# A rounding step and a product moved from VectorE to ScalarE in a kernel's last stage, with a new order of its turn

## The chip, the cores and the metric

The kernel runs on one core of a Trainium2 chip. The time is the device time of one execution in microseconds (us). The engines are called by the profile's names: PE (TensorE), DVE (VectorE), ACT (ScalarE), POOL (GpSimd), SP (SyncE, which only issues transfers here).

## The reference, cut to what matters

Four residual layers, each fed by a group norm without weights, run over 32 images of 128 channels by 32 x 32:

```python
x = x + conv3x3(gn(x))                # layer 0
x = x + mamba_block(gn(x))            # layer 1: two passes, forwards and backwards
x = x + attention(gn(x))              # layer 2
x = x + circuit(gn(x))                # layer 3
...
# layer 2: means over rows and columns go through two small mambas to maps
result_h = sigmoid(a_h) * x_y
result_w = sigmoid(a_w) * x_x
out1 = _c1x1(concatenate([result_h, result_w], axis=1), adjust_w)
return x * out1
...
# layer 3: a small quantum circuit on four angles per pixel
xq = xf @ pre_w.T + pre_b
z = _simulate(xq, q_weights)
out = z @ post_w.T + post_b
```

A group of the norm has four channels. Its mean and variance are means over four partitions, got with a small product by a constant matrix (`self.group`). The circuit's state is written with sines of sums of the angles, so its work per pixel is: a product to turns, the whole part of the turns taken off (rounding), a sine, a product, a square, a product.

## The kernel before, in words

`run()` (L1068) has three stages. `images()` (L1116) does layers 0 and 1, image after image, in an order written out by tables (`PLACES`, `DECAYS`, `LEADS`): 128 scan directions of 32 steps each. At an image's end (L1245) `total` writes the new image to a DRAM tensor `x2`, `rows` and `columns` sum it, three statistics stages give the norm of layer 2, and `means` (L1278) scales the sums on ACT (L1286) and sends the small tile `st` (72 columns) to the DRAM tensor `stats` (L1289). The tiles of one image, `st` among them, come from the pool `img`; the weights from the pool `par`. Both pools end with this stage.

Then `run()` opens a pool `maps` on the right side of SBUF, loads all of `stats` into the tile `means` (L1106, on SP's queue), and calls `attention()` (L1343): two more scan directions over the means of all images at once. Its parameters lie in a pool `par2`, and are loaded in `Mamba.__init__` (L309): five loads per mamba on ACT's queue (L320), one weight and four rows on SP's (L322, L325), products of them on DVE (L328), an exponential on ACT (L331). Its first products on PE are those of `project` (L396), which read `means`; ACT reads their result (L403, recorded at L960).

`tail()` (L1606) is the last stage: the multiplication of layer 2 by its maps, and layer 3. It is a pipeline written by hand: the list `order` (L1757) names 22 parts with the number of turns by which each lags behind the first. Turn j runs the parts in the list's order, each on image j less its lag, so 32 images take 40 turns. The instructions of an engine run in the order in which they are written. By engine, in the list's order:

- PE: `adjust(0)`, `angles`, `states`, `mean`, `adjust(1)`, `outputs`, `variance`
- DVE: `end` (two passes), `root` (one column), `adjusted(0)`, `sums` (three), `less` (one column), `rounded` (two passes, L1719 and L1720), `spread` (three of one column, L1685 to L1687), `turns`, `adjusted(1)`
- ACT: `normed`, `squares`, `normal`, `sines`
- POOL: `total` (L1670), `root`'s power (L1697), `outer` (two products over 128 x 1024, rh at L1644 and rw at L1645)
- SP: the load of the next image (L1639), and the output at `end` (L1753)

Inside one turn `mean` needs `sums`, `spread` needs `mean`, `variance` needs `spread`. `root`, in the next turn, needs `variance`; `less` and `normal` follow it. `rounded` needs `angles`, `turns` needs `rounded`, `sines` needs `turns`. `total` needs `adjusted(1)` of the turn before. The two halves of `adjust` have a PSUM bank each; `q`, `psi`, `mean` and `variance` have one each.

Of the kernel before, what the change touches and what calls it, by code (L numbers as in the profile page):

```python
# [12 lines left out]
F32 = mybir.dt.float32  # L13
BF16 = mybir.dt.bfloat16
AF = mybir.ActivationFunctionType
ALU = mybir.AluOpType
# [3 lines left out]
P = 128  # L20
S = 32
HW = S * S
L = S + 3
# [3 lines left out]
MAGIC = 12582912.0  # L27
# [912 lines left out]
class Kernel:  # L940
# [127 lines left out]
    def run(self):  # L1068
        tc, nc, d = self.tc, self.nc, self.d
        with ExitStack() as ctx:  # L1070
            cst = ctx.enter_context(tc.tile_pool(name="cst", bufs=1))
            self.dram = ctx.enter_context(tc.tile_pool(name="dram", bufs=2, space=bass.MemoryType.DRAM))
            cbig = cst.tile([P, 2 * P], F32, name="cbig")
            nc.sync.dma_start(cbig, d["cbig"])
            self.group, self.ident = cbig[:, :P], cbig[:, P:]
            self.sel = cst.tile([3 * DS, DS, P], BF16, name="sel")
            nc.sync.dma_start(self.sel, d["sel"])
            self.half = cst.tile([P, P], BF16, name="half")
            nc.vector.tensor_copy(self.half, self.ident)
            self.ones = cst.tile([P, 1], F32, name="ones")  # L1080
            nc.sync.dma_start(self.ones, d["ones"])
            self.vecs = cst.tile([P, len(VEC)], F32, name="vecs")
            nc.scalar.dma_start(self.vecs, d["vec"])
            self.eps = cst.tile([P, 1], F32, name="eps")
            nc.vector.memset(self.eps, 1e-5)
            self.one = cst.tile([P, 1], F32, name="one")
            nc.vector.memset(self.one, 1.0)
            self.less = cst.tile([P, 1], F32, name="less")
            nc.vector.memset(self.less, -1.0)
            self.part = cst.tile([P, 1], F32, name="part")  # L1090
            nc.vector.memset(self.part, 1.0 / S)
            self.power = cst.tile([P, 1], F32, name="power")
            nc.vector.memset(self.power, -0.5)


            self.stats = self.dram.tile([P, self.n, 2 * L + 2], F32, name="stats", bufs=1)
            self.x2 = self.dram.tile([self.n, P, HW], F32, name="x2", bufs=1)
            with ExitStack() as scans:
                self.work = Work(scans.enter_context(tc.tile_pool(name="work", bufs=1)))
                self.psm = scans.enter_context(tc.tile_pool(name="psm", bufs=2, space=PSUM))  # L1100
                self.psb = scans.enter_context(tc.tile_pool(name="psb", bufs=2, space=PSUM))
                self.psy = scans.enter_context(tc.tile_pool(name="psy", bufs=1, space=PSUM))
                self.images()
                right = ctx.enter_context(tc.tile_pool(name="maps", bufs=1, side="right"))
                self.means = right.tile([P, self.n, 2 * L + 2], F32, name="means")
                nc.sync.dma_start(self.means, self.stats)  # L1106
                self.maps = right.tile([P, self.n, 4 * S], F32, name="maps")
                self.attention()
            self.tail()
# [6 lines left out]
    def images(self):  # L1116
        tc, nc, d = self.tc, self.nc, self.d
        with ExitStack() as ctx:
            par = ctx.enter_context(tc.tile_pool(name="par", bufs=1))
            img = ctx.enter_context(tc.tile_pool(name="img", bufs=2))  # L1120
            w0 = par.tile([P, 9, P], F32, name="w0")
            nc.sync.dma_start(w0, d["w0"])
            nin = par.tile([P, 2, P], F32, name="nin")
# [121 lines left out]
            def end(im):  # L1245
                def inner(c):
                    def run():
                        assert im.outs == 4
                        cs = slice(c * 512, (c + 1) * 512)
                        ps = self.mm()  # L1250
                        nc.tensor.matmul(ps, nin[:, 1], im.o[:, cs], start=True, stop=True)
                        self.later(
                            lambda: nc.scalar.activation(
                                im.o[:, cs], ps, AF.Relu, bias=bn[1][1], scale=bn[1][0]
                            )
                        )
                    return run

                def total():
                    nc.gpsimd.tensor_tensor(im.xt, im.xt, im.o, ALU.add)  # L1260
                    nc.sync.dma_start(
                        self.x2[im.idx : im.idx + 1].rearrange("a p l -> p (a l)"), im.xt
                    )
                    im.st = img.tile([P, 2 * L + 2], F32, tag="means", name="st")
                    nc.gpsimd.memset(im.st, 0.0)

                def rows():
                    nc.vector.tensor_reduce(
                        im.st[:, 3:L], im.xt.rearrange("p (h w) -> p h w", w=S), AX.X, ALU.add
                    )  # L1270

                def columns():
                    nc.vector.tensor_reduce(
                        im.st[:, L + 3 : 2 * L], im.xt.rearrange("p (h w) -> p w h", w=S),
                        AX.X, ALU.add,
                    )

                def means():  # L1278

                    st, mv = im.st, im.st[:, 2 * L :]  # L1280
                    to = img.tile([P, 2], F32, tag="gn_to", name="gn_to")
                    nc.gpsimd.tensor_tensor(to[:, 0:1], mv[:, 1:2], self.part, ALU.mult)
                    nc.gpsimd.tensor_tensor(to[:, 1:2], mv[:, 0:1], mv[:, 1:2], ALU.mult)
                    nc.gpsimd.tensor_tensor(to[:, 1:2], to[:, 1:2], self.less, ALU.mult)
                    both = st[:, : 2 * L].rearrange("p (a l) -> p a l", a=2)[:, :, 3:]
                    nc.scalar.activation(  # L1286
                        both, both, AF.Identity, bias=to[:, 1:2], scale=to[:, 0:1]
                    )
                    nc.sync.dma_start(self.stats[:, im.idx], st)  # L1289

                stats = self.stats_stages(lambda: im.xt, img, lambda: im.st[:, 2 * L :])
                return [
                    *(Stage(inner(c), pe=0.9, act=0.8, takes=True, gap=2 - c) for c in range(2)),
                    Stage(total, pool=2.4, gap=2), Stage(rows, dve=1.3, gap=2),
                    Stage(columns, dve=1.3), *stats, Stage(means, act=0.3, pool=0.6, gap=2),
                ]

            images, ways, plan = [], [], Table(self)
            for j in range(self.n):
                im = Image()  # L1300
# [305 lines left out]
    def tail(self):  # L1606
        tc, nc, d = self.tc, self.nc, self.d
        with ExitStack() as ctx:
# [54 lines left out]
            def adjusted(c):  # L1663
                def run(im):
                    xn = im.xn[:, halves[c][1]]
                    nc.vector.tensor_tensor(xn, xn, im.adj[c], ALU.mult)  # L1666
                return run
# [14 lines left out]

            def spread(im):
                im.mv, im.dv = tile_([P, 2], "gn_mv"), tile_([P, 1], "gn_dv")
                nc.vector.tensor_copy(im.mv[:, 0:1], im.ps[:, 0:1])  # L1685
                nc.vector.tensor_tensor(im.dv, im.ag[:, 0:1], im.mv[:, 0:1], ALU.subtract)  # L1686
                nc.vector.scalar_tensor_tensor(  # L1687
                    im.dv, im.dv, im.dv, im.ag[:, 1:2], ALU.mult, ALU.add
                )
# [7 lines left out]
                nc.gpsimd.tensor_tensor(im.mv[:, 1:2], im.dv, self.power, ALU.pow)  # L1697

            def less(im):
                mv = im.mv  # L1700
                nc.vector.scalar_tensor_tensor(  # L1701
                    mv[:, 0:1], mv[:, 0:1], -1.0, mv[:, 1:2], ALU.mult, ALU.mult
                )

            def normal(im):
                mv = im.mv
                im.x4 = tile_([P, HW], "x4")
                nc.scalar.activation(im.x4, im.xt, AF.Identity, bias=mv[:, 0:1], scale=mv[:, 1:2])

            def angles(im):  # L1710
                im.q = bank("q", 1)
# [5 lines left out]
            def rounded(im):  # L1717
                im.kk = tile_([64, 512], "kk")
                nc.vector.tensor_scalar(im.kk, im.q[:64], wb, MAGIC, ALU.add, ALU.add)  # L1719
                nc.vector.tensor_scalar(im.kk, im.kk, MAGIC, None, ALU.subtract)  # L1720

            def turns(im):
                im.rr = tile_([64, 512], "rr")
# [24 lines left out]
            def end(im):  # L1748
# [7 lines left out]

            order = [  # L1757
                (total, 3), (adjust(0), 2), (end, 8), (normed, 1), (root, 5), (angles, 6),
                (adjusted(0), 2), (states, 7), (squares, 7), (sums, 4), (less, 5), (normal, 5),
                (mean, 4), (outer, 1), (rounded, 6), (adjust(1), 2), (spread, 4), (turns, 6),  # L1760
                (sines, 6), (outputs, 7), (adjusted(1), 2), (variance, 4),
            ]
            with tc.manual_schedule():
                for j in range(self.n + 8):
# [25 lines left out]
```

## Time and profile before

| | us |
|---|---|
| median of 3 runs | 12554.25 |
| lowest and highest | 12554.06, 12565.31 |
| the profiled execution's own time | 12567.35 |
| its span | 12565.6 |
| L1289, last `st` sent | 11987.75 |
| L1106, `means` asked for | 11989.32 |
| first product of the last stage's maps, rh (L1644) | 12255.6 |
| last output issued (L1753) | 12562.0 |

The profile is one execution. Its times count from the start of the span. A line of a timeline has start, duration, engine, source line, operation, output and inputs, and the shape; `xN` says how many instructions were merged. An engine's name with a q (ACTq, SPq) stands for the instructions that it only issues. In the groups' lines the number behind the bar is the idle time of the engine just ahead, with what ended it.

### The profile page before, as it was taken

The numbers are of one execution on the slowest core, as the hardware profiler recorded it, in microseconds if no ns is written. First come the engines' busy times: TensorE is split into PE (matmuls) and PEld (weight loads), VectorE is DVE, ScalarE is ACT, GpSimd is POOL, SyncE is SP. The second block draws the span as 40 slices with busy tenths as digits, with TensorE's granted clock in tenths as the row PEclk, the third lists the DMA queues.
The fourth block names the chain that finished last, engine by engine and source line by source line (L and its number), as shares of the span: only waits on it lengthen the run. The fifth ranks groups of instructions, "written<-read, shape, count | busy, mean of one in ns | idle before, by whom it ended". The sixth has DMA issues, their size and how long they took to land. (4 is left out here: it accounts for less than half of the span.)

```text
span 12565.6 us, 211133 instructions
## 1 busy us (share of the span) xinstructions
PE 12230.3 (97%) x76364; PEld 8662.6 (69%) x76364; DVE 12059.9 (96%) x7702; ACT 11859.4 (94%) x23290; POOL 11992.8 (95%) x6399
## 2 busy tenths in 40 slices
PE   8999999999999999999999999999999999999988
PEld 5777777777777777777777777777777777777642
DVE  8999999999999999999999999999999999999978
ACT  7999999999999999999999999999999999999963
POOL 6999999999999999999999999999999999999966
PEclk9999999999999999999999999999999999999989
DMA  4555555555555555555555555555555555555532
GB/s 139 187 185 185 186 186 186 187 183 187 185 187 185 188 184 184 183 186 187 186 186 186 186 185 185 186 189 184 185 185 186 187 185 186 186 185 184 187 135 108
DMA packets 633949, 2278.48 MB, mean 181 GB/s; under 512 B 77480, under 2 KB 81144, under 8 KB 632776
## 3 DMA queue, kind: packets, MB, share of 16 engines
q1 hardware_dynamic: 630600, 2263.08, 51.8%
q8 instruction: 603, 9.88, 0.3%
q14 instruction: 442, 3.62, 0.1%
q10 hardware_dynamic: 2304, 1.90, 0.1%
HBM read 2221.36 MB, written 43.34 MB: 180 GB/s over the span
## 5 line engine op out<-in xcount | busy, mean ns | idle before, releaser
L882 POOL TENSOR_TENSOR hh<-hh,cc 128x1024 f32<-128x1024 f32 x4160 | 9762.8, 2375 | 210.4 <-DVE hh L873 125.9
L873 DVE TENSOR_TENSOR_SCAN hh<-da,bu 128x1024 f32<-128x1024 f32 x4160 | 9288.0, 2273 | 291.1 <-PE y L918 68.1
L857 ACT ACTIVATE but<-dut,bt 128x128 f32<-128x128 f32 x14936 | 4503.0, 394 | 71.5 <-PE bu L830 71.4
L918 PEld LDWEIGHTS y<-cbig,hh 128*128 128x128 f32 x33280 | 3762.4, 141 | 1164.7 <-issue 973.1
L816 ACT ACTIVATE da<-dt,m_na 128x1024 f32<-128x1024 f32 x4096 | 4448.3, 1143 | 29.0 <-DVE hh L873 23.7
L918 PE MATMUL y<-cbig,hh 128*128 128x128 f32 x33280 | 4359.7, 275 | 58.1 <-POOL hh L882 57.7
L830 PE MATMUL bu<-cbig,but 128*128 128x128 f32 x19368 | 2545.4, 275 | 33.2 <-DVE hh L873 26.7
L830 PEld LDWEIGHTS bu<-cbig,but 128*128 128x128 f32 x19368 | 2200.9, 141 | 220.9 <-issue 128.8
L865 DVE TENSOR_TENSOR bu<-du,bu 128x1024 f32<-128x1024 f32 x1739 | 2104.6, 1210 | 83.6 <-PE bu L837 73.9
L396 PE MATMUL mm<-hpad,m_wc 128*128 128x512 f32 x4096 | 1943.5, 603 | 33.4 <-ACT dt L960 25.0
L396 PEld LDWEIGHTS mm<-hpad,m_wc 128*128 128x128 f32 x4096 | 709.7, 190 | 775.6 <-issue 695.4
L837 PE MATMUL bu<-parts,sel 48*128 48x512 bf16 x3478 | 1052.8, 383 | 42.1 <-DVE hh L873 41.2
L854 POOL TENSOR_TENSOR but<-dut,bt 128x1024 f32<-128x1024 f32 x554 | 1063.2, 1919 | 0.0
L524 POOL TENSOR_TENSOR du<-dt,uc 128x1024 f32<-128x1024 f32 x260 | 615.7, 2368 | 36.7 <-ACT dt L960 36.7
L960 ACT ACT_TABLE_LOAD x477 | 612.0, 1283 | 9.3 <-DMA my_cw<-in_my_cw 1.4
L965 ACT ACT_TABLE_LOAD x470 | 603.0, 1283 | 11.8 <-DMA cbig<-in_cbig 3.6
L1170 PE MATMUL mm<-xpad,w 128*128 128x512 f32 x1152 | 542.8, 608 | 2.7 <-ACT xpad L1155 2.7
L897 PEld LDWEIGHTS y<-m_skip,uc 128*128 128x128 f32 x4096 | 489.3, 194 | 50.4 <-issue 23.9
L897 PE MATMUL y<-m_skip,uc 128*128 128x128 f32 x4096 | 514.5, 279 | 1.0 <-ACT back L937 0.9
L417 PE MATMUL mm<-uc,m_xw 128*128 128x512 f32 x1024 | 497.7, 609 | 0.0
L837 PEld LDWEIGHTS <-sel 48*128 48x128 bf16 x3478 | 193.7, 94 | 409.0 <-issue 289.2
L960 ACT ACTIVATE uc<-mm,m_pv 128x512 f32<-128x512 f32 x512 | 335.0, 686 | 109.0 <-PE mm L396 106.0
(208 smaller groups left out, 7364.8 us busy)
## 6 DMA issues: line engine op xcount, KB each, us to landing
cc<-rows SPq DMA_DIRECT2D x4160, 512.0 KB, 4.1
xt<-in_x SPq DMA_DIRECT2D x32, 512.0 KB, 5.7
x<-xt SPq DMA_DIRECT2D x32, 512.0 KB, 2.9
xt<-x SPq DMA_DIRECT2D x32, 512.0 KB, 3.9
out<-xt SPq DMA_DIRECT2D x32, 512.0 KB, 2.9
rows<-dbl SPq DMA_DIRECT2D x130, 64.0 KB, 3.9
stats<-st SPq DMA_DIRECT2D x32, 36.0 KB, 3.5
means<-stats SPq DMA_DIRECT2D x1, 1152.0 KB, 5.6
```

What stands on the lines that cost most here:

```text
L396: nc.tensor.matmul(self.view(ps), m.wc[:, v, j, h * P : (h + 1) * P], self.taps(j, c), start=(j == 0), stop=(j == 3),)
L816: k.nc.scalar.activation(t, w.dt[h], AF.Exp, scale=w.m.na[:, h, n : n + 1])
L830: k.nc.tensor.matmul(t[:, b * P : (b + 1) * P], but[:, b], k.ident, start=True, stop=True, is_transpose=True,)
L837: k.nc.tensor.matmul(t[:, cs], k.sel[:, n], w.parts[:, cs], start=True, stop=True)
L854: engine.tensor_tensor(t, w.dut[h], each, ALU.mult)
L857: engine.activation(t[:, b], w.dut[h][:, b], AF.Copy, scale=w.bt[:, b, n : n + 1])
L865: k.nc.vector.tensor_tensor(t, w.du[h], t, ALU.mult)
L873: k.nc.vector.tensor_tensor_scan(way(t), way(self.da.pop(i)), way(self.bu.pop(i)), 0.0, ALU.mult, ALU.add)
L882: k.nc.gpsimd.tensor_tensor(t, t, self.cc.pop(i), ALU.mult)
L897: nc.tensor.matmul(self.y[g][: w.bl, b], w.uc[h][:, at], m.skip[:, h], start=(b == 0), stop=False)
L918: k.nc.tensor.matmul(self.y[g][: w.bl, b], t[:, at], k.ident, start=False, stop=(n == DS - 1 and b == w.per - 1), is_transpose=True,)
L960: self.nc.scalar.activation(*args, **kw)
```

## The change

In `tail()`: the second pass of `rounded`, which subtracts the rounding constant again, becomes the part `whole`, an activation on ACT with a constant tile `unmagic` as its bias. `less`, the product of the mean and the reciprocal deviation, becomes an activation on ACT with the latter as its scale; the minus sign moves into `spread`, which now writes the negated mean. `spread` subtracts the mean straight from PSUM. The list has another order: `rounded` and `whole` stand ahead of `less`, and `mean` stands behind `adjust(1)`.

Between the first two stages: the pool `img` is opened ahead of `par`; the last image's `st` is taken from the pool `work`, stays in SBUF, and is copied into `means` by POOL; the load of `means` takes the other 31 images.

```diff
+            self.unmagic = cst.tile([64, 1], F32, name="unmagic")
+            nc.vector.memset(self.unmagic, -MAGIC)
...
-            self.stats = self.dram.tile([P, self.n, 2 * L + 2], F32, name="stats", bufs=1)
+            self.stats = self.dram.tile([P, self.n - 1, 2 * L + 2], F32, name="stats", bufs=1)
...
-                nc.sync.dma_start(self.means, self.stats)
+                nc.sync.dma_start(self.means[:, : self.n - 1], self.stats)
+                nc.gpsimd.tensor_copy(self.means[:, self.n - 1], self.last)
...
+            img = ctx.enter_context(tc.tile_pool(name="img", bufs=2))
             par = ctx.enter_context(tc.tile_pool(name="par", bufs=1))
-            img = ctx.enter_context(tc.tile_pool(name="img", bufs=2))
...
-                    im.st = img.tile([P, 2 * L + 2], F32, tag="means", name="st")
+
+                    pool = self.work if im.idx == self.n - 1 else img
+                    im.st = pool.tile([P, 2 * L + 2], F32, tag="means", name="st")
...
-                    nc.sync.dma_start(self.stats[:, im.idx], st)
+                    if im.idx == self.n - 1:
+                        self.last = st
+                    else:
+                        nc.sync.dma_start(self.stats[:, im.idx], st)
...
-                nc.vector.tensor_copy(im.mv[:, 0:1], im.ps[:, 0:1])
-                nc.vector.tensor_tensor(im.dv, im.ag[:, 0:1], im.mv[:, 0:1], ALU.subtract)
+
+                nc.vector.tensor_scalar(im.mv[:, 0:1], im.ps[:, 0:1], -1.0, None, ALU.mult)
+                nc.vector.tensor_tensor(im.dv, im.ag[:, 0:1], im.ps[:, 0:1], ALU.subtract)
...
             def less(im):
-                mv = im.mv
-                nc.vector.scalar_tensor_tensor(
-                    mv[:, 0:1], mv[:, 0:1], -1.0, mv[:, 1:2], ALU.mult, ALU.mult
-                )
+                im.by = tile_([P, 1], "by")
+                nc.scalar.activation(im.by, im.mv[:, 0:1], AF.Copy, scale=im.mv[:, 1:2])
...
-                nc.scalar.activation(im.x4, im.xt, AF.Identity, bias=mv[:, 0:1], scale=mv[:, 1:2])
+                nc.scalar.activation(im.x4, im.xt, AF.Identity, bias=im.by, scale=mv[:, 1:2])
...
-                nc.vector.tensor_scalar(im.kk, im.kk, MAGIC, None, ALU.subtract)
+
+            def whole(im):
+                nc.scalar.activation(im.kk, im.kk, AF.Identity, bias=self.unmagic)
...
-                (adjusted(0), 2), (states, 7), (squares, 7), (sums, 4), (less, 5), (normal, 5),
-                (mean, 4), (outer, 1), (rounded, 6), (adjust(1), 2), (spread, 4), (turns, 6),
-                (sines, 6), (outputs, 7), (adjusted(1), 2), (variance, 4),
+                (adjusted(0), 2), (states, 7), (squares, 7), (sums, 4), (rounded, 6), (whole, 6),
+                (less, 5), (normal, 5), (outer, 1), (adjust(1), 2), (mean, 4), (spread, 4),
+                (turns, 6), (sines, 6), (outputs, 7), (adjusted(1), 2), (variance, 4),
```

## The prediction

> **What bounds the kernel now.** I read the page first, then the stretches of the last part, then the chain, then one turn in order of time. The page:
>
> ```profile
> span 12565.6 us, 211133 instructions
> PE 12230.3 (97%) x76364; PEld 8662.6 (69%) x76364; DVE 12059.9 (96%) x7702; ACT 11859.4 (94%) x23290; POOL 11992.8 (95%) x6399
> ```
>
> These shares describe the scans, which the change doesn't touch. The last part runs from 12255 us to the end, 310 us or 2.5% of the span. Its stretch (columns: PE, PEld, DVE, ACT, POOL busy, clock, DMA share, GB/s) and the chain that ended last:
>
> ```profile
> 12300.00:12400.00 100.00, 84.22 (x251) 27.58 (x250) 98.37 (x172) 40.69 (x46) 74.50 (x45) 1.00 0.32 116
> ```
> ```profile
> 12437.66 1.21 DVE gn_st L1675 x2
> 12439.10 1.48 DVE gn_mv L1701
> 12440.58 0.67 DVE kk L1719
> 12441.27 1.44 DVE kk L1720
> ```
>
> DVE is full, ACT 60% idle. But a one-column product (L1701) costs as much as a pass over 64x512. The timeline of one turn, DVE and POOL, says why:
>
> ```profile
> 12443.80 0.67 DVE L1666 TENSOR_TENSOR xn<-xn,adj 128x512 f32<-128x512 f32 x1
> 12444.61 2.37 POOL L1670 TENSOR_TENSOR xt<-xt,xn 128x1024 f32<-128x1024 f32 x1 [2.18 <-ACT rr L1729]
> ...
> 12446.93 0.55 POOL L1697 TENSOR_TENSOR gn_mv<-gn_dv,power 128x1 f32<-128x1 f32 x1
> 12447.45 1.92 POOL L1644 TENSOR_TENSOR rh<-maps 128x1024 f32<-128x1024 f32 x1
> ...
> 12447.81 1.57 DVE L1701 SCALAR_TENSOR_TENSOR gn_mv<-gn_mv 128x1 f32<-128x1 f32 x1
> ...
> 12449.31 1.92 POOL L1645 TENSOR_TENSOR rw<-maps 128x1024 f32<-128x1024 f32 x1
> ...
> 12450.07 1.44 DVE L1720 TENSOR_SCALAR kk<-kk 64x512 f32<-64x512 f32 x1
> ...
> 12451.80 0.22 DVE L1687 SCALAR_TENSOR_TENSOR gn_dv<-gn_dv,gn_ag 128x1 f32<-128x1 f32 x1
> ```
>
> L1701 ends at 12449.38, when rh ends (12449.37); L1720 ends at 12451.51, just behind rw (12451.23). In the drain, where POOL makes no rh and rw, the same two take 0.11 and 0.42 us (the tiles' own rows: L1720 min 418 ns, median 1439). So a DVE operation with two SBUF inputs, or the plain SBUF pass of L1720, waits until the POOL product under way is over; L1666, L1675, L1719 with PSUM or one SBUF input don't. The turn is a loop: rw ends; L1720 ends 0.28 later; the three small ones to L1687's end at 12452.02 take 0.51; L1724 and the second L1666 end 1.25 later; 0.13 on, POOL's total starts (12453.40). That is 2.17. From total, pow starts after 2.32, rh after another 0.52, rw after 1.86 and runs 1.92: 6.62. 2.17 + 6.62 = 8.79, and total's starts from 12286.32 to 12523.76 are 27 intervals of 8.79. The one wait whose removal shortens a turn is the wait behind rw.
>
> **The tail, part by part.** Removed from DVE: L1701 (1.56) and L1720 (1.44). Added on ACT: the pass over 64x512, 0.62 (sine 0.63, square 0.59 for that shape), and the product, 0.30 (L857, a copy with a column as scale, is 0.394 at 128 columns; less 0.1 for the columns). ACT per turn: 1.23 + 0.59 + 0.62 + 0.30 + 1.24 + 0.63 = 4.6, against 3.7. Only what lies on the loop counts. The copy of the mean becomes a product from PSUM of the same size, and dv now subtracts PSUM, one SBUF input: both at nothing different. But L1687 keeps two SBUF inputs (dv, ag). It is 0.22 alone; in the ramp, where L1686 or L1687 met a running rw, each took up to 1.76 to 1.78. Does it meet one now? I walk the new order with total at 0, rw then at 4.70 to 6.62. On PE the variance product of the turn before goes out when L1687 ends, which the walk must return. Take that at -1.39: adjust(0) runs -1.09 to 0.80 (1.9, from 12443.52 to 12445.42), angles 0.98 and states as much to 2.76, adjust(1) 1.89 to 4.65, then mean. DVE reads mean some 0.45 later (0.42 from its start, at the ramp's first mean) at about 5.1, dv 0.18 later, L1687 near 5.5: 0.8 inside rw. It ends with rw at 6.63. 6.63 less one turn is -1.39 again if the turn is 8.02, so the walk closes. The loop is then 0.02 + 1.25 + 0.13 + 6.62 = 8.02. PE has 7.3 per turn, ACT 4.6, DVE's own work 5.9: they fit. rounded ends near 4.0, whole on ACT 4.7, turns needs it at 6.6: 1.9 us of cover. If it went, each us of lateness would be a us of turn.
>
> Moving mean behind adjust(1) makes DVE wait at spread; queued behind it are turns, adjusted(1) and, through that, POOL's total: just the loop counted. Outputs stand behind mean on PE, and variance behind outputs; before L1687 ends both have time.
>
> Sum: 27 turns by 0.77 = -20.8. Ramp: the interval before them, 7.60, loses the old waits and falls to POOL's own 6.6: -1.0. Drain: the first turn without rh and rw is 6.41 and PE's 7.1 becomes its length, +0.7; the last images meet no POOL product, so ACT's 0.62 and 0.30 replace 0.42 and 0.11, with four crossings of 0.09 between engines and a place behind another image's whole: +1.6. Tail: -19.5.
>
> A rule against the change: the Trainium skill, "ScalarE: Activation LUTs", Rules for kernel authors, wants add and mul on VectorE, not ScalarE. By operation length it is right here: 0.42 against 0.62, 0.11 against 0.30, so 27 turns by 0.4 = +11 us. By the row at its place, 1.44 and 1.56 with the wait, it is wrong. I take the row.
>
> **The hand-over at 11990 us.** Before:
>
> ```profile
> 11975.57 0.36 ACTq L320 DMA_DIRECT2D mx_zw<-in_mx_zw  x1
> ...
> 11987.28 0.44 ACT L1286 ACTIVATE st<-st,gn_to 128x64 f32<-128x64 f32 x1 [2.30 <-POOL gn_to L1284]
> ...
> 11989.28 1.28 ACT L960 ACT_TABLE_LOAD   x1
> ```
>
> means is asked for at 11989.32 on SP, lands 5.6 later, and PE's first projection (L396) starts at 11995.26, its first reader on ACT at 12000.71. The load of 31 images may now go out some 12 us earlier and leaves that path; a POOL copy of 72 columns (some 0.3) brings the last. Behind the load on SP's queue stand loads that it delays by 0.33. But mx_zw's issue waited for the last ACT reader of par (11975.54), though its own place was w0's, read long before: new tiles wait for the whole old pool. With img at the bottom, the attention's parameters wait for img's last reader, L1286, until 11987. So ten parameter loads, table loads and the two exponentials on ACT, hidden until now, follow L1286. Before they took 9.4 us to 11984.98 and 2.8 more after L1286, 12.2; late waits behind other work fall away. From 11986.8 that gives 11998 to 11999 for the first reader instead of 12000.71; PE has by then two of its four projections done (two PSUM buffers) and starts the third at 11998.7 to 12000 instead of some 12004.4. From 0 (all of the chain again exposed) to -6.5 (PE alone, four blocks of 3.5 to 5.4 from 11988.3); I take -4.5. The constant's memset at the start: 0.1, under the first loads.
>
> Sum -24.0. Against the profiled execution's 12567.35 (span 12565.6) that gives 12543; the median of the runs shown is 13.1 lower, and from 12554.25 it is 12530.
>
> **Rivals.** (a) L1687 escapes rw, because mean comes 0.8 us sooner than walked. Then PE bounds, at 7.3 per turn: 27 by 0.7 more, 12511. Against it: PE's 0.98s and 1.89s are steady in every turn. (b) The hand-over gives nothing or loses up to 5 (weights late): 12535 to 12540. For it: all 16 us of the old preparation are moved. (c) Slower: table loads. The product uses Copy between Identity and Sine; the stage had one load for Sine, Identity and Square (L1729, 1283 ns, once), and no row shows Copy beside Sine. If it forced two loads a turn: by the rows a load is 1.28 with no gap behind it (11987.74 to 11989.03), ACT 4.6 + 2.6 = 7.2, under 8.02, costing some 9 in the drain, 12539. The skill, same page, What ACT_TABLE_LOAD costs, has 2.66 with its drain: 4.6 + 5.3 = 9.9, 27 by 1.1 = +30, drain +10 to +20, hand-over -4.5: 12590 to 12600. It decides when ACT's turn passes 8.79, two loads above 4.2 us. The page's Table sets section counts copy among the functions in every set, so unlikely.
>
> **How the numbers follow.** About 0.2% (25 us) is what a measurement of this kernel can tell. Forecast 0.70, split by the hand-over and by the spread of runs (11 us among three) about 12529: 0.38 faster, 0.32 same. (a) 0.08, faster. (b) 0.16, same. (c) 0.06, slower. Faster 0.46, same 0.48, slower 0.06. Range 12508 to 12548: (a) below; (b) plus spread above; (c) left out.
>
> **What would show it.** Total's starts 8.0 apart; L1687's line at some 1.1 us, ending with rw; whole at 0.62, product 0.3 on ACT, one table load; PE busy 91% there; L396 before 11990, mx_zw after 11986. Turns of 7.3 or of 9 and more, or an L1687 of 0.22, would prove the walk wrong.

## The result and the profile after

| | before | after |
|---|---|---|
| median, us | 12556.1 (14 runs) | 12530.36 (14 runs) |
| lowest and highest | 12542.28, 12568.96 | 12524.02, 12545.64 |
| profiled execution, its span | 12567.35, 12565.6 | 12530.45, 12528.7 |

The ratio of after to before is 0.9978, with a 95% interval from 0.997 to 0.9986. The forecast was 12530.0 us. The page's head, and a stretch of the last stage (its length, then the columns PE, PEld, DVE, ACT, POOL, granted clock of PE, DMA share, GB/s):

```profile
span 12528.7 us, 211028 instructions
PE 12221.0 (98%) x76364; PEld 8667.2 (69%) x76364; DVE 12006.1 (96%) x7639; ACT 11889.0 (95%) x23355; POOL 11992.6 (96%) x6400
```
```profile
12300.00:12400.00 100.00, 90.34 (x274) 32.12 (x274) 86.78 (x163) 55.92 (x75) 81.76 (x50) 1.00 0.36 127
```

In this stretch DVE fell from 98 to 87 busy us of 100, and ACT rose from 41 to 56. No engine is full, though PE, at 90, is near it. The chain that ended last:

```profile
12299.22 1.47 DVE gn_dv L1696
...
12307.24 1.46 DVE gn_dv L1696
```

The two DVE waits that the chain of before held (1.48 and 1.44) are gone. A new one stands there: L1696, the last of `spread`'s three one-column operations, comes back every 8.02 us. Part of one turn, in order of time (POOL's last line is the next `total`):

```profile
12402.23 0.72 ACT L1729 ACTIVATE kk<-kk,unmagic 64x512 f32<-64x512 f32 x1 [0.44 <-DVE kk L1726]
...
12403.01 1.90 POOL L1653 TENSOR_TENSOR rw<-maps 128x1024 f32<-128x1024 f32 x1
...
12403.48 1.45 DVE L1696 SCALAR_TENSOR_TENSOR gn_dv<-gn_dv,gn_ag 128x1 f32<-128x1 f32 x1
12404.86 0.73 DVE L1733 SCALAR_TENSOR_TENSOR rr<-q,wb,kk 64x512 f32<-64x512 f32 x1
...
12406.32 2.37 POOL L1678 TENSOR_TENSOR xt<-xt,xn 128x1024 f32<-128x1024 f32 x1 [1.41 <-ACT rr L1738]
```

L1696 starts 0.47 into rw and ends at 12404.93; rw ends at 12404.91. `whole` (L1729) is done at 12402.95 and its reader (L1733) starts at 12404.86, so its cover is 1.9 us. No row says that L1696 waits for POOL. Its length says it, against 0.22 in the drain, where POOL makes no rw, and so does an end that falls on rw's.

The hand-over:

```profile
11975.37 0.44 ACT L1291 ACTIVATE st<-st,gn_to 128x64 f32<-128x64 f32 x1 [10.67 <-POOL gn_to L1289]
11975.84 0.37 ACTq L320 DMA_DIRECT2D mx_zw<-in_mx_zw  x1
11975.84 1.14 DVE L328 TENSOR_TENSOR mx_wc<-mx_uw,mx_cw 128x256 f32<-128x256 f32 x3 [1.82 <-ACT st L1291]
...
11976.37 10.00 PE L396 MATMUL mm<-means,mx_wc 128*128 128x512 f32 x16 [2.55 <-DVE mx_wc L328]
...
11985.83 0.69 ACT L960 ACTIVATE uc<-mm,mx_pv 128x512 f32<-128x512 f32 x1
...
11986.57 7.32 PE L396 MATMUL mm<-means,mx_wc 128*128 128x512 f32 x16 [0.20 <-ACT uc L960]
...
11993.92 0.69 ACT L960 ACTIVATE uc<-mm,mx_pv 128x512 f32<-128x512 f32 x1 [2.86 <-PE mm L396]
```

The parameters' loads now start behind the last image's scaling, as walked. PE's first projection starts at 11976.37, when the product `mx_wc` (L328) is there, which waited for that scaling; POOL's copy (0.50) ends at the same time. PE then works through the four projections (32 products) until 11993.88 and stands for 0.4 us in between.

**Where the 36.9 us between the two spans went.** Three stretches of both traces:

| us | before | after | difference |
|---|---|---|---|
| last ReLU of the images to the fourth read of a projection on ACT | 36.45 | 30.00 | -6.45 |
| from there to the first rh (attention) | 244.4 | 245.2 | +0.8 |
| first rh to the end | 309.96 | 289.54 | -20.4 |

That is -26.1, beside -25.7 between the medians. The other 10.8 us arose ahead of the first row: that ReLU starts at 11974.76 in the one profile and at 11963.92 in the other. The image stage does the same work in both, and in the profiles of the nine kernels below, which share it, the same ReLU starts between 11957.8 and 11971.8, with before's hand-over (11958.2 to 11962.6) no later than with after's; so I take it for the spread of executions. What goes with it is PE's granted clock, which the traces show at 0.50 for stretches of 3.4 us and more. Summed up ahead of that ReLU, it stood there for 184 us before and for 160 after; in the eleven profiles the earliest ReLUs (11957.8 and 11958.2) have 133, the latest below (11971.8) 178. Which of the two is the cause no run shows. A reader of the two spans alone would have credited the 10.8 us to the change.

### The profile page after: what moved, and what is told of

Same layout as the page of the kernel before. It is cut to its first block, busy times and chain, and to the rows that moved or that the text cites. A ratio compares the mean times of both kernels' runs of the same rounds, so it can differ in the third digit from the quotient of the medians.

```text
span 12528.7 us, 211028 instructions
## 1 busy us (share of the span) xinstructions
PE 12221.0 (98%) x76364; PEld 8667.2 (69%) x76364; DVE 12006.1 (96%) x7639; ACT 11889.0 (95%) x23355; POOL 11992.6 (96%) x6400
```

## The experiments

My theory was the prediction's: the stage is a loop through the DVE operation that waits for rw, and nothing else in the edit matters there. The rivals stand in the expectations. Turn means the interval between two starts of `total`; last stage, from the first rh to the end. Of `less` alone, `whole` alone and the order alone there is one run each, so they are read by their turns; the others have several, and a ratio to before with its interval.

**The two halves of the change.** The last stage's edits alone (before's images and hand-over), and the hand-over's alone:

> The changed last stage with the hand-over of before (pool par at the bottom, all of stats loaded). Theory (two independent parts): turns of 8.02 as in the changed kernel, the last stage some 20 us shorter than before, the first projection again waits for the load of means; ratio to before 0.9984, 0.9 to 1.6 us per thousand around it from scatter. Rival (the hand-over carries a good part of the gain): the last stage 10 us shorter at most.

> The last stage of before with the new hand-over (img at the bottom, last tile kept on chip). Theory: last stage unchanged at 310 us with turns of 8.79; from the last image's second ACT pass to the fourth read of the first projections some 6 us less than before; ratio 0.9995. Rival (the hand-over is worth nothing, because the parameters now wait): 0 us there, ratio 1.000.

Measured: the last stage's part 12538.57 us, ratio 0.9983 (0.9976 to 0.999), turn 8.02, last stage 288.7, hand-over 36.9. The hand-over's part 12549.64 us, ratio 0.999 (0.9982 to 0.9998), turn 8.79, last stage 309.65, hand-over 29.9. The halves do not touch each other: each profile shows the new value of its own stretch and the old of the other. The hand-over's gain in the median is barely clear of noise; its 6.5 us in the profile repeats.

**The old order with the moved operations.**

```diff
-  (sums, 4), (rounded, 6), (whole, 6), (less, 5), (normal, 5), (outer, 1), (adjust(1), 2), (mean, 4), (spread, 4),
+  (sums, 4), (less, 5), (normal, 5), (mean, 4), (outer, 1), (rounded, 6), (whole, 6), (adjust(1), 2), (spread, 4),
```

> The changed kernel with the two parts on ACT, but the list in the order of before (mean ahead of adjust(1), less and normal ahead of whole). Theory (the turn is set by where the last DVE operation with two SBUF inputs, in spread, meets POOL): mean is there earlier, that operation meets rh instead of rw and ends with it, then turns waits for whole, which stands behind normal on ACT: walked at 7.64 per turn, last stage 281 us against 289.6, so 9 us faster than the changed kernel. Rival (the new order is what makes the moves pay): turns longer than 8.02, up to 8.8.

Measured: 12524.61 us, ratio 0.9972 (0.9963 to 0.9981), turn 7.62, last stage 283.6. Lines of its turn, and lines of the chain that ended last:

```profile
12384.45 1.90 POOL L1652 TENSOR_TENSOR rh<-maps 128x1024 f32<-128x1024 f32 x1
...
12385.97 0.40 DVE L1696 SCALAR_TENSOR_TENSOR gn_dv<-gn_dv,gn_ag 128x1 f32<-128x1 f32 x1
...
12387.75 0.74 DVE L1733 SCALAR_TENSOR_TENSOR rr<-q,wb,kk 64x512 f32<-64x512 f32 x1 [1.38 <-ACT kk L1729]
```
```profile
12385.25 0.38 PE mean L1689 x2
...
12390.69 0.69 DVE xn L1674
12391.38 1.21 DVE gn_st L1683 x2
...
12392.61 0.22 DVE gn_ag L1685
...
12392.88 0.38 PE mean L1689 x2
```

With `mean` early, L1696 meets the end of rh, waits 0.2, and rw not at all. `turns` (L1733) does wait 1.38 for `whole`, as expected, but 7.64 was walked along the wrong path: `whole` is not in the chain. The chain closes over PE and DVE, once a turn: `mean`, the second half of `adjust`, `outputs`, `variance`, the first half of `adjust` for the next turn, then on DVE `adjusted(0)` and `sums`, and `mean` again. PE stands 0.24 for DVE's sums ahead of `mean`. The work behind `whole` has some room: DVE idles 0.22 for PE ahead of `adjusted(0)`. The new order costs 0.40 us of turn against the old one with the same moves, and 6.0 us of the last stage. In the medians that isn't clear: the two intervals overlap.

**The wait itself taken away.** The new order, but the difference stays in PSUM, in an unused column of the mean's bank, so that L1696 has one SBUF input left:

```diff
-  nc.vector.tensor_tensor(im.dv, im.ag[:, 0:1], im.ps[:, 0:1], ALU.subtract)
-  nc.vector.scalar_tensor_tensor(im.dv, im.dv, im.dv, im.ag[:, 1:2], ALU.mult, ALU.add)
+  nc.vector.tensor_tensor(im.ps[:, 1:2], im.ag[:, 0:1], im.ps[:, 0:1], ALU.subtract)
+  nc.vector.scalar_tensor_tensor(im.dv, im.ps[:, 1:2], im.ps[:, 1:2], im.ag[:, 1:2], ALU.mult, ALU.add)
```

> The changed kernel, with the difference of spread written to PSUM, so that the operation after it reads one SBUF input and one PSUM input. Theory (two SBUF inputs make it wait for POOL's product under way): it takes 0.2 us instead of 1.45, turns fall to PE's own 7.3, last stage 269 us, ratio to before 0.9967. Rival 1 (the operation is long for another reason, its place behind mean or its scalar operand): it stays at 1.4 and turns at 8.0. Rival 2 (PE's or POOL's loop is nearer than walked): 0.2 us, but turns of 7.6 and more.

Measured: 12500.48 us, ratio 0.9955 (0.9942 to 0.9969), turn 7.20, last stage 265.6. Its interval lies below that of the change (0.997 to 0.9986).

```profile
12349.44 1.91 POOL L1653 TENSOR_TENSOR rw<-maps 128x1024 f32<-128x1024 f32 x1
...
12350.33 0.22 DVE L1696 SCALAR_TENSOR_TENSOR gn_dv<-mean,gn_ag 128x1 f32<-128x1 f32 x1
```
```profile
12280.00:12380.00 100.00, 100.00 (x307) 35.70 (x305) 80.08 (x182) 62.20 (x83) 92.40 (x56) 1.00 0.42 148
```

The same operation on the same engine, 0.89 into a running rw, takes 0.22, in all 32 images from 222 to 224 ns. So it isn't POOL's running that costs time, but the second SBUF input. That is what the Trainium skill ("SBUF — State Buffer", Who interferes with whom) says: a DVE instruction with two SBUF inputs and a POOL instruction that reads SBUF exclude each other, and one with a single SBUF input, outside the modes that take both ports, does not.

The column that the operation takes as its scalar moved to PSUM with it; L1701 of before has no such column and waited as well. PE is busy throughout, the chain that ended last lies on PE alone, and the turn is PE's. The last stage is 24 us shorter than with the change.

**Both together, PSUM and the old order.**

> The kernel after with both the PSUM operand and the old order of the list. My theory: the old order's turn is set by the second rounding pass, which stands behind the normalisation pass on ScalarE (7.62 with SBUF operands, where L1696 took only 0.40); the PSUM operand takes 0.2 off an operation that is not on that path, so the turn stays at 7.6, the last stage near 283 and the time near 12522. Then the new order is the better one, by 0.4 a turn, once no VectorE operation meets rw. Rival: the old order's turn hung on the 0.40 all the same; then it falls to PE's 7.2, as with the new order, and the time to some 12500.

Measured: 12525.29 us, ratio 0.9972 (0.9962 to 0.9982), turn 7.62, last stage 283.4. L1696 takes 0.22 and it makes no difference, since that operation isn't on the old order's path. The expectation named `whole` as what sets the turn; the outcome alone can't tell that from `mean`, but the chain is again the one through `sums` and `mean`. The four turns:

| | old order | new order |
|---|---|---|
| L1696 with two SBUF inputs | 7.62 | 8.02 |
| L1696 with one | 7.62 | 7.20 |

Each order has its own limit. In the old one PE stands for `mean`. The new one puts `mean` behind the second half of `adjust`, where PE doesn't stand for it, and pays with the meeting of L1696 and rw; once that is gone it is 0.4 better than the old. It also runs `whole` earlier. No run moves `mean` and `whole` one without the other, so how much of the 0.4 each brings stays open.

**One part at a time, on the kernel before.** `less` alone to ACT (with `spread`'s two lines), `whole` alone, the order alone:

> Before, with only the product less on ACT (and the two lines of spread that go with it); rounding whole on DVE, order and hand-over of before. Theory (a turn is as long as the loop from one end of rw to the next, and only waits behind POOL's products on it count): the second rounding pass now comes early enough to wait behind rh instead of rw, and the last operation of spread takes its place behind rw: turns of 8.02, the same as the changed kernel although 0.4 to 1.4 us more per turn stay on DVE. Rival (DVE's load sets the turn, so each move pays its own share): about half of the gain, turns of 8.4.

> Before, with only the second rounding pass on ACT; less on DVE, order and hand-over of before. Theory: less still waits behind rh, the second operation of spread (two SBUF inputs) waits behind rw, and whole, behind normal on ACT, comes 0.1 to 0.3 us later still: turns of 8.3. Rival (DVE's load): 8.79 less the pass's 1.44, 7.4.

> Before, with the list in the new order only; both parts stay on DVE, hand-over of before. Theory: rounding's second pass now comes ahead of less and waits behind rh, less ends behind rw or close to it, and spread follows: turns of 8.5, a gain of 0.25 per turn. Rival (the order is what pays, the moves are beside the point): 8.0.

Measured: turns of 8.20, of 8.27, and of 8.70 or 8.85; last stages of 295.2, 298.6 and 309.3; times 12540.7, 12538.64 and 12553.56. With `less` alone, the plain pass stays on DVE:

```profile
12379.30 1.92 POOL L1644 TENSOR_TENSOR rh<-maps 128x1024 f32<-128x1024 f32 x1
...
12380.39 1.11 DVE L1718 TENSOR_SCALAR kk<-kk 64x512 f32<-64x512 f32 x1
12381.17 2.10 POOL L1645 TENSOR_TENSOR rw<-maps 128x1024 f32<-128x1024 f32 x1
...
12381.66 1.62 DVE L1687 SCALAR_TENSOR_TENSOR gn_dv<-gn_dv,gn_ag 128x1 f32<-128x1 f32 x1
```

The pass gets its turn when rh ends (12381.22) and works on to 12381.50; meanwhile rw has begun, and takes 2.10 instead of 1.91. L1687 then waits for that longer rw. So 8.20 is the walked 8.02 with 0.18 added: the exclusion works in both directions, which the expectation had left out. With `whole` alone the wait behind rw is L1688's (1.11), and 8.27 is as walked. With the order alone there are two kinds of turn, here one of each:

```profile
12382.94 1.91 POOL L1645 TENSOR_TENSOR rw<-maps 128x1024 f32<-128x1024 f32 x1
12383.08 2.05 DVE L1720 TENSOR_SCALAR kk<-kk 64x512 f32<-64x512 f32 x1
...
12391.02 1.09 DVE L1720 TENSOR_SCALAR kk<-kk 64x512 f32<-64x512 f32 x1
12391.80 2.08 POOL L1645 TENSOR_TENSOR rw<-maps 128x1024 f32<-128x1024 f32 x1
12392.04 1.85 DVE L1701 SCALAR_TENSOR_TENSOR gn_mv<-gn_mv 128x1 f32<-128x1 f32 x1
```

In 16 of the 27 turns, those of 8.70, it goes as expected: the pass waits behind rh, `less` behind rw. I had put that turn at 8.5, again without the time by which the pass holds rw up (2.08 to 2.10 instead of 1.91). In the other 11, of 8.85, the pass begins behind rw's start, in the rows above by 0.14, and waits for rw's end. These are the turns in which PE's granted clock is 0.50 for 1.9 us or more; in the others it is so for 1.5 at most. Either way next to nothing is gained. The gain of the last stage comes from the two moves, and each alone brings most of it (0.59 and 0.52 of the 0.77), because either leaves one operation at rw's end.

**What remains of the hand-over.** On the PSUM kernel, the parameters' pool waits tile by tile, not for the whole old pool, and the ten loads go out on SP, not on ACT:

```diff
-  nc.scalar.dma_start(getattr(self, key), d[f"{name}_{key}"])
+  (nc.scalar if name == "m1" else nc.sync).dma_start(getattr(self, key), d[f"{name}_{key}"])
...
-  par = ctx.enter_context(tc.tile_pool(name="par2", bufs=1))
+  par = ctx.enter_context(tc.tile_pool(name="par2", bufs=1, reuse_waits="tile"))
```

> The kernel with the difference in PSUM (turns of 7.2), and the attention's ten parameter loads issued on SP, with waits for the single tiles whose place they take instead of for the whole pool img. Theory (after the change the hand-over is bound by the parameters behind the last image's scaling on ACT): ACT is free right after that scaling; from the last image's second pass to the fourth read of the first projections 27 us (26 to 28) instead of 30.0; last stage as before it, 265.6; ratio to before 0.9953. Rival (the table loads, or PE at its lower clock, bind it): 30 us as now.

Measured: 12504.88 us, ratio 0.9958 (0.9945 to 0.9972), hand-over 26.8, turn 7.20.

```profile
11968.50 1.10 DVE L328 TENSOR_TENSOR mx_wc<-mx_uw,mx_cw 128x256 f32<-128x256 f32 x3
11969.03 16.23 PE L396 MATMUL mm<-means,mx_wc 128*128 128x512 f32 x32 [0.67 <-PE mm L1056]
...
11970.15 0.44 ACT L1291 ACTIVATE st<-st,gn_to 128x64 f32<-128x64 f32 x1 [10.91 <-POOL gn_to L1289]
...
11974.79 0.69 ACT L960 ACTIVATE uc<-mm,mx_pv 128x512 f32<-128x512 f32 x1 [2.78 <-PE mm L396]
```

The size came as expected, but not from the parameters behind the scaling on ACT. From the end of L1291 to the first read is 4.2 us, where after had 10.0, yet in after nearly all of that lay under PE's projections, between which PE stood for 0.4. The 3.2 us are two other terms. PE starts 10.6 us behind the last ReLU instead of 12.4, since `mx_wc` (L328) no longer waits for L1291; and the four projections take 16.2 instead of 17.5, without the 0.4 and with fewer products at the half clock (of the 32, 5 stand 0.7 to 1.0 apart instead of 0.44; in after 7 stand 0.6 to 1.0 apart). In the medians it can't be told from the kernel without it. The two edits of this run were not tried apart; by the rows the wait that is gone is one for a tile's place, not for a load.

## Why the prediction was right, step by step

**The turn as a loop through rw's end**: right, and the main result. 27 intervals of 8.02, as walked. The walk had `mean` ready later than it was: L1696 starts 0.47 into rw, not 0.8, and so takes 1.45, not 1.1. Its end is rw's end in either case, so the error cost nothing. Taking the wait away (7.20) shows that this operation, and no other, held the turn at 8.02. That the forecast lies 0.4 us from the median is in part luck: the change brought 25.7 us, not 24.0, and the median of before came out 1.9 above that of the three runs it was taken from.

**Rival (a), PE as the bound**: its price was right (7.3 walked, 7.20 measured), its condition not met. It needed the second SBUF input gone, not an earlier `mean`.

**The moved operations**: the product 0.28 (0.30 forecast), the pass 0.72 (0.62). The estimate came from sine and square; the sine of the same shape is 0.63 in this trace as well, and why this pass is longer no run shows. At 1.9 us of cover it didn't matter. In the old order the cover is gone (`turns` starts as soon as `whole` ends), and even there the pass had 0.22 to spare.

**"Moving mean behind adjust(1) makes DVE wait at spread; ... just the loop counted"**: the count was right, but the prediction took the order as given and never priced the old order with the same moves. That would have shown that the new place of `mean` carries L1696 from rh's end into rw, for 0.40 a turn, and that it spares PE a wait, which pays only once the meeting is gone.

**Ramp and drain**: walked at -1.0, +0.7 and +1.6, together +1.3. Measured: the first three intervals -1.3; first rh to first `total` 9.2 to 10.66, +1.45, which wasn't walked; the last interval 6.41 to 6.78, +0.37; last `total` to the end 35.4 in both, so the +1.6 for ACT's longer operations didn't come. Together +0.5. The last stage's -20.4 stands against -19.5, close because these misses nearly cancel. What the walk left out is PE's granted clock, which falls to 0.50 in the ramp and the drain. The last 27.6 us ahead of the last output:

```profile
12497.40:12525.00 27.60, 23.25 (x44) 5.22 (x42) 13.83 (x25) 10.62 (x17) 1.10 (x2) 0.50 0.19 76
```

The kernel before shows the same there (PE busy 23.45 of 27.4 us, clock 0.50). At that clock the four products of `angles` take 1.92 us instead of 1.05, and the chain runs through PE image after image, through `whole` once only. Where the half clock begins 11.0 us behind the last `total` (the hand-over's part alone) instead of 4.4 (before), the way from it to the end takes 33.2 instead of 35.4. The ramp's +1.45 goes with it as well: behind the first rh PE has 6.8 us at 0.50 in after, 3.4 before; with the last stage's part alone it has 3.4, and the way to the first `total` is 9.70.

**The rule against the change**, add and mul on VectorE: by length of operation it holds here too (0.42 and 0.11 against 0.72 and 0.28), and the turn is 0.77 shorter all the same. Leaving both on DVE with a PSUM operand was not tried.

**Hand-over**: right in mechanism, -6.45 against -4.5, the PE-only end of its bounds. From the end of the scaling to the first read took 10.0 where 11.2 to 12.2 was walked, so that it held PE up by only 0.4. Counted from the last ReLU, PE starts 8.05 us sooner, and its projections take 1.6 longer (17.5 instead of 15.9), for that 0.4 and because 7 of their products, not 4, fall at the half clock. In detail, 1.07 came ahead of the scaling: before, POOL's `xt` sum ran beside DVE's products of the parameters (L1260 at 2.58, 2.34 after) and the statistics queued behind them. The rest, 5.4, came behind it.

**Rival (c), table loads in each turn**: refuted. The last stage has one load, with Copy, Identity, Sine and Square in it.

## What to carry to other kernels

Where a one-column operation takes as long as a pass over a tile, compare its end with the ends on the other engines: the row names no releaser, but an end that coincides in every turn does. Before moving such an operation to another engine, ask whether one input can be left in PSUM; here that was worth 30 us in the median, 24 of them in the last stage by the profile, where the whole change had brought 26. Before saying what sets a turn, follow the chain through it once round: a wait that a row shows (`turns` for `whole`) need not be on it. And walk each order with each set of operations: the better order with the wait was the worse one without it.

## What the runs showed of the hardware that was not expected

- The exclusion holds POOL up too: rw took 2.08 to 2.10 us instead of 1.91 when it began while DVE's plain SBUF pass was at work. With the order alone both lengths stand in one trace, 2.08 to 2.10 where the pass came first and 1.91 where rw did.
- A one-column operation is held as long as a large one: 1.45 us for 128 x 1, against 0.22 with one input in PSUM. The wait is the rest of POOL's product, whatever the size of the DVE operation.
- An activation with a bias column over 64 x 512 took 0.72 us, where the sine of that shape took 0.63.
- PE's granted clock fell to 0.50 in the hand-over, the ramp and the drain, and with the order alone inside the turns. The four products of `angles` took 1.92 us there instead of 1.05.
- Executions of one kernel spread over some 20 to 30 us (before: 12542.28 to 12568.96), and between two profiles nearly 11 us of that lay in a stretch that the change didn't touch. The spread goes with the mean granted clock: of 33 executions of before, the seven at 0.988 took 12563.6 to 12571.2 us, the four at 0.990 12550.4 to 12555.5.
